# A gated recurrence over columns: 1 − z straight from ScalarE, the state as a product less a product, and one group of matmuls one place later

## The chip, the cores and the metric

The kernel runs on one core of one Trainium2 chip. The metric is the time of one execution in microseconds (us), as the device measures it; the median of several runs counts. A profiled execution is one further run whose every instruction is recorded. Engines are PE (TensorE: matmuls; PEld are its weight loads), DVE (VectorE), ACT (ScalarE), POOL (GpSimd) and SP (SyncE, which issues most of the DMAs).

## What is computed

The input is an image `x` of shape (4, 64, 256, 256): batch, channels, height, width. Layer 0 is a gated convolution block (with Fourier products over 8 × 8 patches) added to `x`. Layer 1 normalizes the result in groups and runs a gated recurrent cell over the columns of the image; its output is added too. The change is in layer 1 only:

```python
def _gru_cell(x, h, w_ih, w_hh, b_ih, b_hh):
    gi = x @ w_ih.T + b_ih
    gh = h @ w_hh.T + b_hh
    i_r, i_z, i_n = jnp.split(gi, 3, axis=-1)
    h_r, h_z, h_n = jnp.split(gh, 3, axis=-1)
    r = jax.nn.sigmoid(i_r + h_r)
    z = jax.nn.sigmoid(i_z + h_z)
    n = jnp.tanh(i_n + r * h_n)
    return (1.0 - z) * n + z * h
...
def step(prev_col, cur_col):
    nb = jnp.concatenate([pad, prev_col, pad], axis=1)
    x = jnp.concatenate([nb[:, :-2], nb[:, 1:-1], nb[:, 2:]], axis=-1)
    new = _gru_cell(x..., cur_col..., w_ih, w_hh, b_ih, b_hh)
    return (new, new)
```

Two things are unusual. What the cell calls `h` is the current column of the normalized image, and what it calls `x` is the previous column's new state with its upper and lower neighbour (three taps). So the 255 steps hang on each other through `w_ih`, while the products with `w_hh` need only the image.

## The kernel before

Layer 0 fills the first 4.37 ms and is not touched. Layer 1 then takes 256 columns `w` in order (the loop at the end of the kernel). All values are fp32. Two images of 64 channels lie on the 128 partitions, and two such pairs lie side by side, so a column is a tile of 128 partitions × 2 × 256 rows.

A column is cut into two ranges of its 256 rows, part 0 and part 1 (`parts`). The border between them moves up by one row with every column, from 144 down to 113, and jumps back every 32 columns. So the three taps of part 0 need only part 0 of the previous column's state; part 1 needs both parts, and at a jump part 0 does too.

`column` issues PE's work. `own` is a product of the column itself with `w_hh`, four matmuls on the four quadrants of the array (eight records in the trace: each fp32 matmul is recorded twice); `taps` is the three products with the previous state, twelve matmuls (24 records). The results lie in four PSUM tags with one buffer each, two banks per buffer, which makes all eight banks: `hr` (r; pshr in the profile), `ni` (the taps' share of n; psni), `hz` (z; pshz), one buffer per range, and `hn` (the column's own share of n; pshn), one buffer for the whole column, which both ranges read. PE's order in a column is: pshn for all 256 rows; then for each range pshr (own, taps), psni (taps), pshz (own, taps).

`state` issues the rest for each range, in this order. ACT: r into tile `g` (sigmoid of pshr), then `normalize` of half a column that is eight columns ahead (`xn<-raw`), then tanh into tile `n`, then z (sigmoid of pshz). DVE: `n` = (pshn + bias) · r (SCALAR_TENSOR_TENSOR n<-pshn), `n` = psni + n, and behind the tanh three steps: g = xn − n, g = g · z, st = g + n. The state `st` is what the next column's taps read. The tiles `g`, `n`, `z` have a pool of two buffers for each range (`gk`).

Program order is kept on every engine (`InOrder`), and each engine takes its queue strictly in order: an instruction that waits holds up all behind it. After a column, POOL adds its state to the image for the output (`add`, raw<-raw,st); SP issues the loads of later columns, the transposed copies `xt<-xn` of the normalized columns, and the stores. ACT computes sigmoid as a function of scale · input + bias, with the sum of two biases in the small tile `b_rz`.

Of the kernel before, what the change touches and what calls it, by code (L numbers as in the profile page):

```python
# [11 lines left out]
AF = mybir.ActivationFunctionType  # L12
ALU = mybir.AluOpType
# [3 lines left out]
B, C, W, H = 4, 64, 256, 256  # L17
# [145 lines left out]
def tile_conv_then_gru(  # L163
# [17 lines left out]
    nc = InOrder(tc, tc.nc)  # L181
# [84 lines left out]
    nc.scalar.dma_start(bias_sb, bias.rearrange("a o n -> (a o) n"))  # L266
    b_rz = const.tile([P, 2], F32, tag="b_rz", name="b_rz")
    nc.vector.tensor_tensor(b_rz, bias_sb[:, 0:2], bias_sb[:, 3:5], ALU.add)

    st1 = const.tile([P, NBLK, 2], F32, tag="st1", name="st1")
    with ExitStack() as s:
# [18 lines left out]
        z = big.tile([P, NP, NS], F32, tag="z", name="z")  # L292
# [424 lines left out]
    with ExitStack() as s:  # L717
        rawp = s.enter_context(tc.tile_pool(name="raw", bufs=3))
        colp = s.enter_context(tc.tile_pool(name="cols", bufs=2))
        gk = s.enter_context(tc.tile_pool(name="gk", bufs=2))  # L720
        ps_g = s.enter_context(tc.tile_pool(name="ps_g", bufs=1, space=PSUM))
        raws, xns, xts, stcols = {}, {}, {}, {}

        def columns(m, w):

            yield m[:, :, w, :].rearrange("(k a) c h -> (a c) k h", k=NPAIR), slice(0, P), 0
            for half in range(2):
                b0 = SLOTS[1][0][half]
                yield m[b0 : b0 + 2, :, w + 1, :].rearrange("b c h -> c b h"), slice(half * C, half * C + C), 1

        def load_columns(w):
            n, i = w // WB, w % WB
            if i == 0:
                raws[n] = rawp.tile([P, 2, WB, H], F32, tag="raw", name=f"raw_{n}")
            for of, at, j in columns(x1, w):
                nc.sync.dma_start(raws[n][at, :, i + j], of)

        def new_columns(n):
            xns[n] = colp.tile([P, 2, WB, H], F32, tag="xn", name=f"xn_{n}")
            xts[n] = colp.tile([P, WB, H], F32, tag="xt", name=f"xt_{n}")  # L740

        def empty_states(n):
            stcols[n] = st = colp.tile([P, 2, WB, H + 2], F32, tag="st", name=f"st_{n}")
            nc.gpsimd.memset(st[:, :, :, 0:1], 0.0)
            nc.gpsimd.memset(st[:, :, :, H + 1 : H + 2], 0.0)

        def normalize(w, slot):
            n, i = w // WB, w % WB
            if i == slot == 0:
                new_columns(n)  # L750
            nc.scalar.activation(
                xns[n][:, slot, i],
                raws[n][:, slot, i],
                AF.Identity,
                bias=sc1[:, w % 2, slot, 0:1],
                scale=sc1[:, w % 2, slot, 1:2],
            )
            if slot and i % 2:

                for half in range(2):  # L760
                    nc.sync.dma_start(
                        xts[n][half * C : (half + 1) * C, i - 1 : i + 1],
                        xns[n][(1 - half) * C : (2 - half) * C, half, i - 1 : i + 1],
                    )

        def add(w):
            n, i = w // WB, w % WB
            nc.gpsimd.tensor_tensor(
                raws[n][:, :, i], raws[n][:, :, i], stcols[n][:, :, i, 1 : H + 1], ALU.add
            )  # L770
            if i % 2:
                for of, at, j in columns(out, w - 1):
                    nc.sync.dma_start(of, raws[n][at, :, i - 1 + j])

        QUARTERS = ((0, 0), (0, 1), (1, 0), (1, 1))
        SKEW = 32

        def parts(w):


            at = H // 2 + SKEW // 2 - (w - 1) % SKEW
            return (0, at), (at, H)

        MAX = H // 2 + SKEW // 2

        def bank_pair(gate, w):
            return ps_g.tile([P, 2, 512], F32, tag=gate, name=f"ps{gate}_{w}")

        def quarters(ps, weights, rhs, start, stop):
            for r, c in QUARTERS:  # L790
                nc.tensor.matmul(
                    ps[c * C : (c + 1) * C, r],
                    lhsT=weights[r * C : (r + 1) * C],
                    rhs=rhs(r, c),
                    start=start,
                    stop=stop,
                    tile_position=(r * C, c * C),
                )

        def column(w):  # L800

            i, xn, xt, st = w % WB, xns[w // WB], xts[w // WB], stcols[(w - 1) // WB]

            def own(ps, gate, h0, h1, stop):

                quarters(
                    ps,
                    wh[:, gate, :],
                    lambda r, c: (xn[:, c] if r == c else xt)[r * C : (r + 1) * C, i, h0:h1],
                    True,  # L810
                    stop,
                )

            def taps(ps, gate, h0, h1, start):
                for t in range(3):
                    quarters(
                        ps,
                        wi[:, 3 * gate + t, :],
                        lambda r, c: st[r * C : (r + 1) * C, c, (w - 1) % WB, h0 + t : h1 + t],
                        start and t == 0,  # L820
                        t == 2,
                    )

            pn = bank_pair("hn", w)[:, :, 0:H]
            own(pn, 2, 0, H, True)
            for part in range(2):
                h0, h1 = parts(w)[part]
                pr, pi, pz = (bank_pair(gate, f"{w}_{part}")[:, :, 0 : h1 - h0] for gate in ("hr", "ni", "hz"))
                own(pr, 0, h0, h1, False)
                taps(pr, 0, h0, h1, False)  # L830
                taps(pi, 2, h0, h1, True)
                own(pz, 1, h0, h1, False)
                taps(pz, 1, h0, h1, False)
                state(w, part, pn[:, :, h0:h1], pr, pi, pz)

        def state(w, part, pn, pr, pi, pz):
            h0, h1 = parts(w)[part]
            i, num = w % WB, h1 - h0
            xn, st = xns[w // WB], stcols[w // WB]
            g = gk.tile([P, 2, MAX], F32, tag=f"g{part}", name=f"g_{w}_{part}")[:, :, 0:num]  # L840
            n = gk.tile([P, 2, MAX], F32, tag=f"n{part}", name=f"n_{w}_{part}")[:, :, 0:num]
            z = gk.tile([P, 2, MAX], F32, tag=f"z{part}", name=f"z_{w}_{part}")[:, :, 0:num]
            nc.scalar.activation(g, pr, AF.Sigmoid, bias=b_rz[:, 0:1], scale=1.0)
            if w + WB < W:
                normalize(w + WB, part)
            nc.vector.scalar_tensor_tensor(n, pn, bias_sb[:, 5:6], g, ALU.add, ALU.mult)
            nc.vector.tensor_tensor(n, pi, n, ALU.add)
            nc.scalar.activation(n, n, AF.Tanh, bias=bias_sb[:, 2:3], scale=1.0)
            nc.scalar.activation(z, pz, AF.Sigmoid, bias=b_rz[:, 1:2], scale=1.0)
            nc.vector.tensor_tensor(g, xn[:, :, i, h0:h1], n, ALU.subtract)  # L850
            nc.vector.tensor_tensor(g, g, z, ALU.mult)
            nc.vector.tensor_tensor(st[:, :, i, 1 + h0 : 1 + h1], g, n, ALU.add)

        for w in range(0, 2 * WB, 2):
            load_columns(w)
        for w in range(WB + 1):
            for slot in range(2):
                normalize(w, slot)
        empty_states(0)
        nc.vector.tensor_copy(stcols[0][:, :, 0, 1 : H + 1], xns[0][:, :, 0])  # L860
        for w in range(W):
            n, i = w // WB, w % WB
            if i == 0 and n + 1 < W // WB:
                empty_states(n + 1)
            if w:
                column(w)
            add(w)
            if i % 2 and w + 2 * WB < W:
                load_columns(w + 2 * WB - 1)
# [54 lines left out]
```

## Time and profile before

| | us |
|---|---|
| median of 3 runs | 5915.67 |
| lowest and highest of them | 5904.98, 5931.4 |
| profiled execution: its own time | 5924.77 |
| profiled execution: span of the trace | 5923.0 |
| first and last DVE step n<-pshn of layer 1, from the start of the span | 4371, 5910 |

Over the whole span PE is busy for 93%, DVE for 69%, ACT for 59% and POOL for 8%; the mean granted TensorE clock is 0.992.

How the lines are read. A row of the timeline has the start from the beginning of the span, the duration (both in us), the engine, the operation, the tile that it writes and those that it reads, the shape, a count, and in brackets the idle time before it and what ended that. All instructions have the line number of one helper (L157), so the tiles' names tell them apart. A row of the waits has who waited for whom, the total in us, the number of times, and the longest. A row of the busy times has the window, its length, then PE, PEld, DVE, ACT and POOL busy time with instruction counts, the granted clock, the share of the DMA engines and GB/s. Matmuls overlap each other, so the pace of PE is read from the starts of successive groups.

### The profile page before, as it was taken

The page shows a single profiled execution, that of the slowest core. Times are in us where ns is not written, and L with a number is a line of the kernel's source. Part 1 is how long each engine was busy: PE and PEld are TensorE (multiplying, and loading weights), DVE is VectorE, ACT ScalarE, POOL GpSimd, SP SyncE. Part 2 cuts the span into 40 slices and gives each one's busy share as a digit, 9 for nine tenths or more (in the row PEclk, how much of TensorE's full clock was granted, in tenths as well). Part 3 has the DMA queues.
Part 4 walks back from the last instruction along what each step waited for, and adds up shares of the span by engine and source line. Part 5 has one row for each costly group of instructions (what it writes and reads, how often), then busy time and mean ns, then how long its engine had stood idle before and what let it go on. Part 6 is the DMA issues. An engine that isn't in the chain of part 4 may idle for free. (4 is left out here: it accounts for less than half of the span.)

```text
span 5923.0 us, 279366 instructions
## 1 busy us (share of the span) xinstructions
PE 5513.2 (93%) x127196; PEld 4736.6 (80%) x127196; DVE 4090.4 (69%) x9592; ACT 3466.3 (59%) x4604; POOL 499.7 (8%) x797
## 2 busy tenths in 40 slices
PE   2999999999999999999999999999979999999998
PEld 1888887888887888778878887887868888888887
DVE  2676776777667777776767776666766666676666
ACT  2556565665655666556566665656645555555555
POOL 0000000000000000000000000000001211121211
PEclk9999999999999999999999999999989999999999
DMA  8455555555555555555555545444454444444442
GB/s 223 132 160 142 154 151 155 152 141 160 151 147 149 157 155 141 147 162 146 153 146 154 145 127 142 133 131 136 123 119 112 113 112 110 113 114 113 111 113 78
DMA packets 561921, 818.09 MB, mean 138 GB/s; under 512 B 41352, under 2 KB 435372, under 8 KB 559676
## 3 DMA queue, kind: packets, MB, share of 16 engines
q1 hardware_dynamic: 520152, 633.59, 39.9%
q0 software_dynamic: 37776, 165.24, 9.5%
q8 instruction: 996, 16.32, 1.2%
q10 hardware_dynamic: 2808, 1.38, 0.1%
q14 instruction: 189, 1.55, 0.1%
HBM read 622.46 MB, written 144.05 MB: 129 GB/s over the span
## 5 line engine op out<-in xcount | busy, mean ns | idle before, releaser
L157 PEld LDWEIGHTS psring<-h,t 100*32 100x32 f32 x40960 | 1334.8, 115 | 300.4 <-issue 176.2
L157 PE MATMUL psring<-h,t 100*32 100x128 f32 x40960 | 1445.7, 274 | 113.0 <-issue 39.4
L157 PE MATMUL psring<-w_sb,xq 64*100 64x128 f32 x24576 | 1396.9, 271 | 58.1 <-POOL xq L157 44.1
L157 PEld LDWEIGHTS psring<-w_sb,xq 64*100 64x100 f32 x24576 | 1352.7, 163 | 117.9 <-issue 48.1
L157 ACT COPY h<-psring 100x1024 f32<-100x1024 f32 x1274 | 1204.0, 1026 | 156.8 <-PE psring L157 150.4
L157 DVE TENSOR_TENSOR pr<-psring,q 128x512 f32<-128x512 f32 (+1 forms) x576 | 463.0, 856 | 299.1 <-PE psring L157 230.8
L157 DVE BATCH_NORM_STATS2 lnst<-z 128x6 f32<-128x64 f32 x4096 | 544.8, 212 | 117.6 <-ACT z L157 117.6
L157 DVE TENSOR_TENSOR z<-z,lnm 128x1024 f32<-128x1024 f32 x512 | 612.6, 1217 | 8.7
L157 ACT COPY q<-psring 128x1024 f32<-128x1024 f32 x256 | 259.2, 1013 | 586.5 <-PE psring L157 351.2
L157 ACT ACTIVATE n<-n,bias_sb 128x288 f32<-128x288 f32 (+7 forms) x510 | 259.8, 509 | 572.7 <-DVE n L157 572.7
L157 ACT COPY z<-psring 128x2048 f32<-128x2048 f32 x128 | 238.9, 1866 | 463.3 <-PE psring L157 458.3
L157 PE MATMUL psring<-pr,g_sb 32*64 32x512 f32 x8192 | 497.5, 602 | 5.9 <-issue 5.7
L157 ACT ACTIVATE y<-psring,ln_sb 128x512 f32<-128x512 f32 x512 | 371.9, 780 | 199.7 <-PE psring L157 196.0
L157 DVE COPY h<-psring 100x1024 f32<-100x1024 f32 x262 | 320.3, 1223 | 193.5 <-PE psring L157 189.4
L157 PE MATMUL psni<-st,wi 64*64 64x144 f32 (+7 forms) x12240 | 440.9, 270 | 7.4 <-issue 6.7
L157 PE MATMUL pshr<-st,wi 64*64 64x144 f32 (+7 forms) x12240 | 434.0, 270 | 13.4 <-DVE st L157 12.9
L157 PE MATMUL pshz<-st,wi 64*64 64x144 f32 (+7 forms) x12240 | 439.4, 270 | 3.9 <-issue 3.5
L157 DVE TENSOR_TENSOR g<-xn,n 128x288 f32<-128x288 f32 (+7 forms) x510 | 217.4, 426 | 325.5 <-ACT n L157 325.5
L157 POOL TENSOR_TENSOR raw<-raw,st 128x512 f32<-128x512 f32 x256 | 303.4, 1185 | 1212.0 <-DVE st L157 522.0
L157 DVE TENSOR_TENSOR y<-psring,y 128x1024 f32<-128x1024 f32 x256 | 312.2, 1220 | 122.1 <-ACT y L157 118.8
L157 PEld LDWEIGHTS pshr<-st,wi 64*64 64x64 f32 x12240 | 362.1, 133 | 16.5 <-issue 16.0
L157 PEld LDWEIGHTS psni<-st,wi 64*64 64x64 f32 x12240 | 363.1, 133 | 14.3 <-issue 11.4
(97 smaller groups left out, 6984.0 us busy)
## 6 DMA issues: line engine op xcount, KB each, us to landing
t<-t_all SPq DMA_DIRECT2D x768, 400.0 KB
xq<-in_xh POOLq DMA_DIRECT2D x128, 800.0 KB, 4.6
xr<-in_x SPq DMA_DIRECT2D x256, 256.0 KB
x<-xr SPq DMA_DIRECT2D x256, 256.0 KB
seen<-in_x POOLq DMA_DIRECT2D x192, 256.0 KB, 4.1
raw<-x SPq DMA_DIRECT2D x128, 256.0 KB
raw<-x SPq DMA_DIRECT2D x256, 128.0 KB
xt<-xn SPq DMA_DIRECT2D x256, 128.0 KB
```

The source lines that it names most:

```text
L157: return self.tc.keep_in_program_order(got(*args, **kwargs))
```

## The change

- ACT computes z' = 1 − z in place of z: the sigmoid of the negated sum (scale −1, and a bias that one more small DVE instruction negates once, at the start).
- ACT's order in a range becomes r, normalize, z', tanh (z' ahead of tanh).
- DVE's last three steps of a range become g = (z' − 1) · xn, which reads no result of the tanh; n = n · z'; st = n − g.
- On PE, pshn is issued behind the two groups of pshr of part 0 and ahead of its psni. The count of PE, DVE and ACT instructions in a column stays as it was. The first DVE step of part 0 now waits for PE as well as for ACT, since pshn is written after pshr.

```diff
     nc.vector.tensor_tensor(b_rz, bias_sb[:, 0:2], bias_sb[:, 3:5], ALU.add)
+    nc.vector.tensor_scalar(b_rz[:, 1:2], b_rz[:, 1:2], -1.0, None, ALU.mult)
...
             pn = bank_pair("hn", w)[:, :, 0:H]
-            own(pn, 2, 0, H, True)
             for part in range(2):
...
                 own(pr, 0, h0, h1, False)
                 taps(pr, 0, h0, h1, False)
+                if part == 0:
+                    own(pn, 2, 0, H, True)
                 taps(pi, 2, h0, h1, True)
...
             nc.vector.tensor_tensor(n, pi, n, ALU.add)
+
+            nc.scalar.activation(z, pz, AF.Sigmoid, bias=b_rz[:, 1:2], scale=-1.0)
             nc.scalar.activation(n, n, AF.Tanh, bias=bias_sb[:, 2:3], scale=1.0)
-            nc.scalar.activation(z, pz, AF.Sigmoid, bias=b_rz[:, 1:2], scale=1.0)
-            nc.vector.tensor_tensor(g, xn[:, :, i, h0:h1], n, ALU.subtract)
-            nc.vector.tensor_tensor(g, g, z, ALU.mult)
-            nc.vector.tensor_tensor(st[:, :, i, 1 + h0 : 1 + h1], g, n, ALU.add)
+            nc.vector.scalar_tensor_tensor(g, z, -1.0, xn[:, :, i, h0:h1], ALU.add, ALU.mult)
+            nc.vector.tensor_tensor(n, n, z, ALU.mult)
+            nc.vector.tensor_tensor(st[:, :, i, 1 + h0 : 1 + h1], n, g, ALU.subtract)
```

## The prediction

> **What bounds it now.** I read the page's chain first, then the waits, then the timeline of one column on each engine, and last the busy times of the stage. Only layer 1's recurrence is touched: 255 columns, which fill the trace from 4371 us to 5910 us.
>
> ```profile
> DVE 17%; PE 6%; ACT 4%; issue 3%; DMA 0%; DVEq 0%; SPq 0%; ACTq 0%; POOLq 0%
> ...
> 5000.00:5300.00 300.00, 279.75 (x9185) 254.74 (x9188) 209.28 (x500) 177.52 (x400) 60.33 (x64) 1.00 0.41 113
> ```
>
> The whole-span chain is mostly DVE although PE is the busiest engine. In the stage (second row: PE, PEld, DVE, ACT, POOL busy, then granted clock) PE is 93% busy, DVE 70%, ACT 59%. The waits name the circle:
>
> ```profile
> ACT n L157 <- DVE n L157: 572.7, 510, 1.9
> DVE g L157 <- ACT n L157: 325.5, 510, 0.9
> PEld pshn L157 <- DVE n L157: 134.3, 227, 1.0
> PE pshn L157 <- DVE n L157: 79.1, 207, 0.7
> ```
>
> Tanh waits for DVE in all 510 ranges, DVE for tanh in all 510, and the first product of a column (pshn) waits for DVE. DVE's timeline, from the second range of one column to the first of the next:
>
> ```profile
> 5071.15 0.48 DVE L157 SCALAR_TENSOR_TENSOR n<-pshn,bias_sb,g 128x262 f32<-128x262 f32 x1
> 5071.73 0.43 DVE L157 TENSOR_TENSOR n<-psni,n 128x262 f32<-128x262 f32 x1
> 5072.80 0.43 DVE L157 TENSOR_TENSOR g<-xn,n 128x262 f32<-128x262 f32 x1 [0.64 <-ACT n L157]
> 5073.34 0.43 DVE L157 TENSOR_TENSOR g<-g,z 128x262 f32<-128x262 f32 x1
> 5073.81 0.43 DVE L157 TENSOR_TENSOR st<-g,n 128x262 f32<-128x262 f32 x1
> 5074.15 0.47 DVE L157 SCALAR_TENSOR_TENSOR n<-pshn,bias_sb,g 128x248 f32<-128x248 f32 x1
> ```
>
> The next range's first DVE step follows the state's last one without a pause, although its r had ended at 5073.73 (last ACT fence: 5073.26 + 0.47). So DVE is a closed ring: five steps and the tanh, start to start 0.58 + 0.53 (to tanh at 5072.26) + 0.54 (tanh to DVE) + 0.54 + 0.47 + 0.34 = 3.00 us for this range, 2.95 with the other one, 5.95 for a column; the starts of this step over all columns have a median distance of 5.95 too. PE follows it:
>
> ```profile
> 5071.68 0.43 PE L157 MATMUL pshn<-xn,wh 64*64 64x256 f32 x1 [0.35 <-DVE n L157]
> ...
> 5072.16 0.27 PE L157 MATMUL pshr<-xn,wh 64*64 64x124 f32 x1
> ...
> 5073.86 0.81 PE L157 MATMUL pshz<-st,wi 64*64 64x124 f32 x24
> 5074.49 0.27 PE L157 MATMUL pshr<-xn,wh 64*64 64x132 f32 x1
> ...
> 5075.40 0.85 PE L157 MATMUL psni<-st,wi 64*64 64x132 f32 x24
> ...
> 5077.62 0.43 PE L157 MATMUL pshn<-xn,wh 64*64 64x256 f32 x1 [0.34 <-DVE n L157]
> ```
>
> From 5071.68 to 5075.40 groups follow each other with nothing between: 3.72 us. What is left of the column (ni 0.68, z's own 0.23 and taps 0.68, by the like groups of the second range) is 1.59. PE needs 5.31 us for a column and takes 5.94. About 0.63 us is slack given back by the wait of pshn.
>
> **The change, part by part.** *State.* The subtraction and its dependent multiply go; in their place stands (z' − 1)·xn, which needs z' = 1 − z and xn but not tanh. Behind the tanh two steps are left. The ring becomes 0.58 + 0.53 + 0.54 + 0.47 + 0.34 = 2.46 us for a range, 4.92 a column, or 5.0 with 0.07 for the second wait that the first range's step now has (PE and ACT; 0.07 is the pause of 0.11 before g<-g,z, which waits for two, less 0.04 before st, which waits for one). The new step runs in DVE's present idle time: DVE can issue 0.34 after the start of n<-psni (5072.07), and tanh's result comes at 5072.80, so 0.73 is free. Its duration has no row. Nearest are 0.48 (the same operation from PSUM), 0.43 (products in SBUF) and 0.52 (the page's smaller groups: the same operation on lnm, 256 elements); I take 0.48. It costs nothing up to 0.8. Uncovered it would cost 0.4 to 0.5 a range, and the ring would be back near 5.9.
>
> *z' before tanh.* A scale of −1 on the same operation costs nothing by these rows. What changes is the queue: tanh and r of the other range stand behind z', which waits for the last product of its range.
>
> ```profile
> 5072.26 0.51 ACT L157 ACTIVATE n<-n,bias_sb 128x262 f32<-128x262 f32 x1 [1.25 <-DVE n L157]
> 5072.68 0.46 ACT L157 ACTIVATE z<-pshz,b_rz 128x262 f32<-128x262 f32 x1
> 5073.26 0.47 ACT L157 ACTIVATE g<-pshr,b_rz 128x248 f32<-128x248 f32 x1
> 5075.24 0.50 ACT L157 ACTIVATE n<-n,bias_sb 128x248 f32<-128x248 f32 x1 [1.02 <-DVE n L157]
> ```
>
> The first range's pshz ends at 5073.86 + 0.81 = 5074.67 and its tanh starts at 5075.24: 0.57 of idle ACT for a step that issues in 0.36. So z' fits ahead of tanh now.
>
> *n of the column itself behind r.* Alone it buys nothing, since DVE sets the pace. Together with the shorter ring, the wait for the PSUM pair that pshn shares between columns gets 0.85 us of PE work (r's products) in front of it.
>
> *What is late next: PE.* I lay a column of 5.31 us out from r's start (0): r ends issuing at 0.85, n 1.33, ni 1.97, z 2.81, second r 3.72, ni 4.40, z 5.31; a result is usable about 0.25 later (a group of taps is 0.81 long while the next starts after 0.63, and 0.07 passes before ScalarE starts where r waits for it alone). z' starts 3.06, tanh 3.42, product 3.96, state 4.43 to 4.85; the second range's first step 4.77, n 5.35 to 5.78, tanh 5.92 (behind z' at 5.56), product 6.46, state 6.93 to 7.36, which is 2.05 of the next column; its first step follows at 1.96, n at 2.54 to 2.97, ahead of tanh at 3.42. It closes with 0.35 to spare. PE never waits: state of the first range needed at 5.52, there at 4.85; of the second at 3.04, there at 2.05; n's pair needed at 6.16, read by 5.24.
>
> *Elsewhere.* The extra step on b_rz (0.16 us, once) follows DVE's 44.3 us wait for the bias. No DMA moves; SP's own waits in the stage are 423 us for POOL and 373 for ACT, so its queue stands a column 0.6 shorter. POOL's addition (1.1 to 1.3 us of a column) starts 0.13 after the second state's end, so it can overlap the first range's new step. Had that to stand until the addition's end, 1.41 after the state's, the product would start 0.24 late and the ring be 5.24, still under PE's 5.31. [...]
>
> *Sum.* 5.95 − 5.31 = 0.64 over 254 column distances: 163 us. Not all comes in. Some fifty PE groups start 0.2 to 1.4 us late in the middle of a product, about 24 us in all, of which the slack now swallows some 17: the distances sum to 1536 against 254 × 5.955 = 1513, and seven columns where the ranges' border jumps back (every 32; 2.2 us waiting for the second state, before and after) take 16 of that 23. Minus 17, and 2 for the transposed copy's rare waits: 144 to 146 us. Own time 5924.8 − 146 = 5779; it lies 9 above the median of the three runs (5915.7), so I predict 5770.
>
> **Rivals.** *PE does not reach its own pace (0.12):* the ring stays at 5.4 to 5.5, if the new step takes 0.8 or more or stands behind POOL, or handoffs cost more than shown. The 0.35 to spare speaks against it, the missing row for it. 5.45 a column: 36 us less, 5806.
>
> *The new step is not hidden (0.05):* if z' always comes too late, DVE does it behind tanh: 2 × (2.46 + 0.48) = 5.88, a gain of 18 us, 5898: no change. The 0.57 us of idle ACT speaks against it.
>
> *Clock (0.08, slower):* TensorE at half its clock, as here:
>
> ```profile
> 4563.69:4567.10 3.41, 3.41 (x66) 3.41 (x60) 0.97 (x2) 1.26 (x3) 0.74 (x1) 0.50 0.13 40
> ```
>
> Such windows follow PE's longest pauses (the 2.2 us of a border jump), three in this stage. With PE as the bound a column takes 5.31 / c: the gain is gone at a mean clock of 0.89 and it turns to a loss below. A third of the time at half clock, c = 0.83, gives 6.4 a column: +114 us, 6030. Against it: 1.00 in the stage, and in layer 0 with PE as dense as it would be here. [...]
>
> **Numbers.** Forecast 0.75, its own range 5742 (all 163 come in, less the 11 by which the lowest run lies under the median) to 5800; partial 0.12; no change 0.05; slower 0.08. Up to 5865 the range holds the partial case too, as far as 5.7 a column. A measurement of this kernel can tell about 0.5% from no change.
>
> **What would show it.** Right: the distance of columns 5.3 to 5.4; pshn's wait for DVE gone; DVE's new step inside its old idle time, two steps after tanh; ACT n waiting for its turn behind z rather than for DVE; PE near 98% in the stage. Wrong: columns near 5.9 with the new step behind tanh, pshr waiting for st in ordinary columns, or a clock below 0.95.

## The result: 0.8% faster, under a third of what was forecast

| | us |
|---|---|
| before, median of 4 runs (lowest, highest) | 5914.34 (5904.98, 5931.4) |
| after, median of 4 runs (lowest, highest) | 5872.74 (5863.04, 5877.1) |
| ratio after to before, 95% interval | 0.9921 (0.9902 to 0.9941) |
| profiled execution of after: its own time, its span | 5869.95, 5868.2 |
| mean distance of columns in layer 1, before and after | 6.048, 5.870 |

The medians lie 42 us apart; 146 were forecast. (The ratio is the one on record; the quotient of the two medians is 0.9930, inside its interval.) The two profiled executions differ by 55 us. The 254 distances between the first DVE steps of successive columns sum to 1536 us before and 1491 after, so 45 of the 55 lie in the recurrence; 9 more lie ahead of layer 1, which started at 4371 us before and at 4362 after, where only one small step at the start was changed. The granted clock is 0.994.

The chain of the page of after, by engine, and below it the busy times of the stage (columns as for before):

```profile
PE 33%; issue 2%; DMA 1%; DVE 1%; ACT 1%; SPq 0%; POOLq 0%; ACTq 0%; DVEq 0%
```

```profile
5000.00:5300.00 300.00, 277.99 (x9328) 264.73 (x9324) 211.55 (x508) 182.29 (x408) 61.73 (x66) 1.00 0.42 116
```

PE has taken DVE's place on the chain, as the prediction said. But in the 300 us it worked off only 1.5% more records than before (9328 and 9324 against 9185 and 9188), and its busy time even fell, from 279.75 to 277.99 us: the forecast wanted columns of 5.48 us in the mean in place of 6.05, 9% less. The waits of after, from 4400 to 5850 us:

```profile
ACT z L157 <- PE pshz L157: 505.0, 493, 2.7
...
PE pshz L157 <- issue: 28.7, 53, 1.2
PE pshr L157 <- issue: 28.6, 59, 1.2
...
PE psni L157 <- issue: 21.6, 30, 1.7
PE pshr L157 <- DVE st L157: 13.4, 7, 1.9
...
ACT n L157 <- DVE n L157: 6.0, 26, 0.6
```

The old circle is open. Tanh waits for DVE 26 times instead of at every range, pshn waits for DVE once (0.2 us), and ScalarE stands in z' and waits for PE's last product. PE waits for a state only at the seven jumps of the border. What it does wait for is "issue", that is, for nothing that the profile can name: 79 us in these three rows. In the same window of before they came to 14:

```profile
PE psni L157 <- issue: 6.7, 14, 0.9
PE pshz L157 <- issue: 5.8, 13, 1.2
...
PE pshr L157 <- issue: 1.2, 3, 0.5
```

The timeline of DVE and ACT in one range:

```profile
5067.51 0.50 DVE L157 SCALAR_TENSOR_TENSOR n<-pshn,bias_sb,g 128x272 f32<-128x272 f32 x1
5068.10 0.44 DVE L157 TENSOR_TENSOR n<-psni,n 128x272 f32<-128x272 f32 x1
5068.79 0.49 ACT L157 ACTIVATE z<-pshz,b_rz 128x272 f32<-128x272 f32 x1 [1.08 <-PE pshz L157]
5069.17 0.51 ACT L157 ACTIVATE n<-n,bias_sb 128x272 f32<-128x272 f32 x1
5069.31 0.44 DVE L157 SCALAR_TENSOR_TENSOR g<-z,xn 128x272 f32<-128x272 f32 x1 [0.76 <-ACT z L157]
5069.72 0.44 DVE L157 TENSOR_TENSOR n<-n,z 128x272 f32<-128x272 f32 x1
5070.20 0.44 DVE L157 TENSOR_TENSOR st<-n,g 128x272 f32<-128x272 f32 x1
```

The second row of DVE ends at 5068.54, tanh starts at 5069.17, and between them lies z' with its wait for PE (1.08 us). The new step (0.44) runs beside the tanh, and two steps follow. All of this is the picture forecast. Only PE isn't at its pace.

### The profile page after: what moved, and what is told of

It is laid out like the page before. It is cut to its first block, busy times and chain, and to the rows that moved or that the text cites. A ratio compares the mean times of both kernels' runs of the same rounds, so it can differ in the third digit from the quotient of the medians.

```text
span 5868.2 us, 278629 instructions
## 1 busy us (share of the span) xinstructions
PE 5479.9 (93%) x127196; PEld 4762.6 (81%) x127196; DVE 4080.5 (70%) x9593; ACT 3475.4 (59%) x4604; POOL 500.8 (9%) x797
## 3 DMA queue, kind: packets, MB, share of 16 engines
q10 hardware_dynamic: 2808, 1.38, 0.1%
## 5 line engine op out<-in xcount | busy, mean ns | idle before, releaser
L157 ACT ACTIVATE z<-pshz,b_rz 128x288 f32<-128x288 f32 (+7 forms) x510 | 242.6, 476 | 519.8 <-PE pshz L157 519.7
L157 PE MATMUL pshr<-st,wi 64*64 64x144 f32 (+7 forms) x12240 | 510.5, 270 | 34.9 <-issue 20.9
L157 PE MATMUL psni<-st,wi 64*64 64x144 f32 (+7 forms) x12240 | 510.4, 270 | 24.4 <-issue 22.4
L157 PE MATMUL pshz<-st,wi 64*64 64x144 f32 (+7 forms) x12240 | 510.8, 270 | 23.1 <-issue 21.9
L157 PEld LDWEIGHTS psni<-st,wi 64*64 64x64 f32 x12240 | 446.5, 133 | 45.5 <-issue 34.4
L157 PEld LDWEIGHTS pshr<-st,wi 64*64 64x64 f32 x12240 | 422.3, 133 | 52.3 <-issue 49.5
L157 PEld LDWEIGHTS pshz<-st,wi 64*64 64x64 f32 x12240 | 424.9, 133 | 37.3 <-issue 36.4
L157 DVE SCALAR_TENSOR_TENSOR g<-z,xn 128x288 f32<-128x288 f32 (+7 forms) x510 | 218.4, 428 | 311.9 <-ACT z L157 310.0
```

The source lines that it names most:

```text
L157: return self.tc.keep_in_program_order(got(*args, **kwargs))
```

## The cause: PE's instructions arrive in blocks

PE's timeline has short pauses in the middle of a product, where the profile names nothing that the next matmul waits for:

```profile
4408.66 0.65 PE L157 MATMUL psni<-st,wi 64*64 64x120 f32 x16
4409.91 0.33 PE L157 MATMUL psni<-st,wi 64*64 64x120 f32 x4 [0.59 <-issue]
```

A group of taps has 24 records; this one stops after its 17th (one lies ahead of the 16 shown) and goes on 0.86 us after the last start. The same happens at other places in other columns. The page of after has what to set beside this: the engines' counts of instructions and the queues' counts of packets.

```profile
PE 5479.9 (93%) x127196; PEld 4762.6 (81%) x127196; DVE 4080.5 (70%) x9593; ACT 3475.4 (59%) x4604; POOL 500.8 (9%) x797
```

```profile
q8 instruction: 996, 16.32, 1.2%
```

PE and PEld together have 254,392 records; 996 transfers of 16.4 KB at 256 records each are 254,976. Queue q8 carries PE's program: its count follows PE's records from kernel to kernel (1012 in split_n, 988 in pair_n, 941 in whole_ni, below). The stage has, from 4400 to 5850 us:

```profile
q8 instruction: 354, 5.80, 1.7%
```

In the records of the single transfers these 354 are 4.09 us apart in the mean, with 256 PE records (matmuls and weight loads) between two starts. Counting a pause as a distance of over 0.25 us between the starts of two PE records, there are 218 (156 us; the text on record of few_stores has 155); 215 of them end 1.0 to 2.0 us after the end of a q8 transfer, at a median of 1.39 us, where chance would put about a quarter there. In the pause shown it is 1.38 us.

The arithmetic: a column has 92 fp32 matmuls, each two matmul and two weight-load records, so 368 records or 1.4375 blocks. At the array's pace of 5.31 us a column (the estimate from the starts of before's groups), a block would have to come every 256 · 5.31 / 368 = 3.69 us. It came every 4.09: 1.4375 · 4.09 = 5.88 us a column, measured 5.87. That product alone proves nothing, since a column's records must arrive in a column's time whatever sets the pace (before: 1.4375 · 4.21 = 6.05). What says more is what is left without the pauses: less an ordinary spacing of 0.06 us for each (nine in ten of all distances are shorter) they are 143 us, and the other 1307 us of the window for 354 blocks are 3.69 us a block, the array's pace. So the pauses account for the whole difference. That the blocks cause them is tested by changing the records and the array's work separately, in the experiments.

The round trip can be read from the pauses. Behind these 215 pauses the next transfer starts no earlier than 1.05 us after PE resumes (median 1.50); a transfer takes 1.09 us in the mean, and the median pause ends 1.39 us after one. That adds up to 3.5 us with the shortest lag and to 4.0 with the median one. Single blocks do come faster: 28% of the distances lie under 3.69 us, but the mean doesn't. No data packet of q1 was in flight at the start of 83 of these transfers; there the median lag was 1.15 us. Where packets were, it was 1.69.

In the texts on record, **F** is this theory: PE gets a block of 256 records every 4 us or so, and the number of records sets the column. **P**, its rival, has PE at the end of its array work and its hand-offs, so that array time taken away or added shows in full and the number of records doesn't matter. **R** is a ring through the states that is still closed. One more rival has no letter: a fixed time that PE needs for each record, wherever the instructions are. The counts of records alone can't tell it from F; the pauses can (narrow, below).

## The experiments

Ratios are to the kernel before, on the same chip, with 95% intervals. "Against after" is the difference to 0.9921, times 5914 us; with both intervals it is uncertain by some 17 us. Means of block and column are from the one profiled execution of each.

| kernel | ratio | 95% | records a column | us a block | us a column |
|---|---|---|---|---|---|
| before | 1 | | 368 | 4.21 | 6.05 |
| after | 0.9921 | 0.9902 to 0.9941 | 368 | 4.09 | 5.87 |
| state_alone | 0.9932 | 0.9913 to 0.9952 | 368 | 4.12 | 5.91 |
| pn_alone | 1.0005 | 0.9991 to 1.0019 | 368 | | 6.09 |
| split_n | 1.0042 | 1.0025 to 1.0059 | 384 | 4.11 | 6.14 |
| pair_n | 0.9876 | 0.9856 to 0.9896 | 360 | 4.12 | 5.79 |
| narrow | 0.9965 | 0.9945 to 0.9985 | 368 | 4.14 | 5.93 |
| lag2 | 0.9899 | 0.9883 to 0.9914 | 368 | 4.06 | 5.83 |
| few_stores | 0.9812 | 0.9781 to 0.9843 | 368 | 3.93 | 5.65 |
| before_few_stores | 1.0005 | 0.9994 to 1.0016 | 368 | | |
| more_stores | 0.9936 | 0.9917 to 0.9955 | 368 | 4.08 | 5.86 |
| whole_ni | 0.9974 | 0.9960 to 0.9988 | 312 | 4.92 | 5.99 |

**Which part brings the gain.** state_alone is after with pshn at the front of the column again:

```diff
+            own(pn, 2, 0, H, True)
             for part in range(2):
...
-                if part == 0:
-                    own(pn, 2, 0, H, True)
```

> The state's three steps and the order of ScalarE as in the changed kernel, but pshn first in the column as before. Theory F (PE now runs out of instructions: it takes them in blocks of 256 records, 16 KB each, on queue q8, and a block comes every 4.09 us on average, so the 368 records of a column take 5.87 us): PE is the bound here too, 5860 to 5890 us, as with both edits. Theory P (PE's own pace or the handoffs set the 5.87 us): the pair of pshn is free at 5.24 us of a column by my layout, so it again costs little: 5860 to 5900. If the place of pshn carried the gain: 5900 or more.

pn_alone is before with pshn moved behind pshr of part 0, and nothing else (the same lines the other way round).

> Only pshn moved behind the products of r of the first range; the state's steps as before. Both theories: DVE's ring of 5.95 us a column still sets the pace, so no gain; with the second wait of the first range's step up to 0.07 us a column longer: 5910 to 5935 us. A gain of 30 or more would say that the ring was not the bound before.

The new order of the state brings the gain, 0.9932; the move of pshn alone brings nothing, 1.0005. Whether the move adds something to the state's change (0.9921 against 0.9932) is within the intervals and stays open.

**More records, the same work.** split_n issues pshn in two halves of 128 rows instead of one of 256, with the same number of columns through the array and 16 records more:

```diff
-                    own(pn, 2, 0, H, True)
+                    own(pn[:, :, 0 : H // 2], 2, 0, H // 2, True)
+                    own(pn[:, :, H // 2 : H], 2, H // 2, H, True)
```

> The changed kernel with each matmul of pshn (256 columns wide) cut into two of 128: the same array work, 16 more PE records in a column, 384 in place of 368 (4.3% more). Theory F: the time of a column grows with the count, 5.87 to 6.12 us, 64 us in all: 5925 to 5940 us. Theory P: the array's work is the same, at most 0.03 us a column for one more group: 5870 to 5882 us.

It lost all that the change had won and more: 1.0042, 72 us against after. F priced 16 records at 64 us, P at 9 or less. The block came at 4.11 us, as in after; only the column has more of them.

**Fewer records, the same work.** pair_n computes pshn for two columns with one set of matmuls 512 wide (the first column alone), into the same two PSUM banks:

```diff
+        lead, k = w % 2 == 0 or w == 1, 1 if w == 1 else 2
+        if lead:
+            pairs[0] = bank_pair("hn", w)[:, :, 0 : k * H].rearrange("p c (k h) -> p c k h", h=H)
+        pn = pairs[0][:, :, 0 if lead else 1]
...
-                if part == 0:
-                    own(pn, 2, 0, H, True)
+                if lead and part == 0:
+                    quarters(
+                        pairs[0],
+                        wh[:, 2, :],
+                        lambda r, c: (xn[:, c] if r == c else xt)[r * C : (r + 1) * C, i : i + k, :],
+                        True,
+                        True,
+                    )
```

> The changed kernel with pshn computed for two columns at once (512 columns wide, every second column): the same array work, 8 PE records fewer a column on average (360 of 368, 2.2%). Theory F: 5.87 to 5.74 us a column, 32 us less than the changed kernel, 0.9865 of the kernel before. Theory P: no change, 0.992.

0.9876, 27 us against after, where F said 32 and P nothing. pair_n is the fastest version of the whole computation here: 5840.78 us beside 5912.92 for the kernel before on its chip.

**The same records, less work.** narrow lets the taps of r and z multiply only the first 64 rows of each range. It leaves part of these products out; the number of matmuls stays, and the array has less work, by the estimate on record 1.31 us in a column:

```diff
-                taps(pr, 0, h0, h1, False)
+                taps(pr[:, :, 0:64], 0, h0, h0 + 64, False)
...
-                taps(pz, 1, h0, h1, False)
+                taps(pz[:, :, 0:64], 1, h0, h0 + 64, False)
```

> The changed kernel, but the taps of r and z cover only the first 64 rows of each range (left out: the other rows' share; ScalarE and DVE read as much as before). Record counts stay at 368 a column, PE's array work falls by 2 x (0.635 - 0.33) + 2 x (0.68 - 0.33) = 1.31 us to 4.0 us a column, under the ring's 5.0. Theory F: a block of 256 records still takes some 3.95 to 4.09 us, so a column 5.65 to 5.87 us: 0 to 60 us less than the changed kernel. Theory P (the array's work is the limit): the ring sets the pace, 5.0 to 5.1 us, about 200 us less.

0.9965: not faster but slower, by some 26 us against after. Its waits in the window from 4400 to 5850 us, and the busy times of the stage:

```profile
PE pshr L157 <- issue: 116.1, 106, 2.4
PE pshz L157 <- issue: 111.3, 111, 2.4
...
PE psni L157 <- issue: 93.2, 88, 2.4
```

```profile
5000.00:5300.00 300.00, 227.54 (x9340) 208.92 (x9341) 212.18 (x505) 180.09 (x405) 60.35 (x63) 0.99 0.42 114
```

The matmuls that are gone from the array have become waits for issue, 321 us in the three rows where after has 79. PE's busy time fell by 50 us in the 300, and its count of records did not move: 18,681 against 18,652 in after. The pauses are now 383 (447 us), and 340 of them end 1.0 to 2.0 us after a block's end. P, which had to gain some 200 us, is out. So is a fixed time per record: without the pauses (424 us less their ordinary spacing) PE takes 2.92 us for a block here (88 records in a us) and 3.69 in after (69), where the means over the whole window are 62 and 63; it is quicker as soon as the instructions are there. F's own band (no loss) was missed as well: the block came at 4.14 us. Why it came a little later than in after isn't explained.

**The state of two columns ago.** lag2 lets the taps read the state of the column before the previous one. It computes another recurrence, with the same instructions and a column more of slack:

```diff
-            i, xn, xt, st = w % WB, xns[w // WB], xts[w // WB], stcols[(w - 1) // WB]
+            i, xn, xt, st = w % WB, xns[w // WB], xts[w // WB], stcols[max(w - 2, 0) // WB]
...
-                        lambda r, c: st[r * C : (r + 1) * C, c, (w - 1) % WB, h0 + t : h1 + t],
+                        lambda r, c: st[r * C : (r + 1) * C, c, max(w - 2, 0) % WB, h0 + t : h1 + t],
```

> The changed kernel, but the taps read the state of two columns ago (another recurrence; left out: the wait for the last state). Every instruction, transfer and shape stays. Theory F: PE is not held by the state, only the seven border jumps go: 10 to 20 us less than the changed kernel. Rival R (the ring through the state and its handoffs holds PE at 5.87 in place of 5.31 us a column): some 140 us less.

0.9899, 13 us against after, in F's band of 10 to 20, though with the 17 us above it can't be told from nothing. R asked for 140 and is out. PE's wait for st at the jumps (13.4 us in after) is gone, and the distances of columns sum to 9 us less; its three rows for issue are 82.5 us, as in after (79). The column takes 5.83 us, so it is no ring through the state that holds it at 5.87.

**What sets the block's time.** few_stores leaves out layer 1's stores of the output, but for the first and last two columns, to see whether the transfers of the program compete with the data:

```diff
-        if i % 2:
+        if i % 2 and (w < 2 or w > W - 2):
```

> The changed kernel with the stores of layer 1's output left out, all but the first and last two columns (256 KB a column of about 640 KB that the DMA queues move). No engine's work changes but SP's. Theory F: the blocks of instructions share the DMA engines with these transfers, so they come sooner; the column falls to 5.4 to 5.6 us, 5760 to 5805 us in all, and PE's pauses of over 250 ns (155 us in the changed kernel) fall to under half. Theory P: nothing that PE waits for has changed, 5865 to 5880 us.

0.9812: 65 us against after. The median of 5820 lies 15 us above F's band, on a chip where before too took 15 us longer than in the runs of the result, and the pauses fell to 97 us, not under half of after's 156; the direction is F's, the size a little short. The block came at 3.93 us instead of 4.09. before_few_stores leaves the same stores out of the kernel before, where the ring sets the pace:

> The kernel before (DVE's ring as the bound), with the same stores left out as in few_stores. Theory F: PE's pauses for instructions lie under the slack of 0.63 us a column, so at most the visible few go: 0 to 15 us less than the kernel before. If it gains as much as the changed kernel did from the same cut (some 60 us), the stores slow something else than PE's instructions, and F loses that support.

1.0005: nothing. So leaving the stores out gained 65 us where PE waited for its supply, and nothing where the ring set the pace. more_stores goes the other way and writes each store a second time, into a spare tensor:

```diff
+    spare = dram.tile([B, C, W, H], F32, tag="spare", name="spare")
...
+            for of, at, j in columns(spare, w - 1):
+                nc.sync.dma_start(of, raws[n][at, :, i - 1 + j])
```

> The changed kernel with each store of layer 1's output issued once more, into a spare tensor (256 KB more a column). Theory F: blocks of instructions come later by about what few_stores gained (3.93 in place of 4.09 us a block), so some 4.2 to 4.3 us and a column of 6.05 to 6.2 us: 45 to 85 us longer than the changed kernel. Theory P: no change.

This was a miss: 0.9936, within the intervals of after, with 4.08 us a block, although the DMA share of the stage rose from 0.42 to 0.57. The share of time without a q1 packet in flight went from 36% to 20% (few_stores: 55%). Between PE's resuming and the next transfer, median lags of 1.15 us without and 1.63 with packets in flight are there in this run as well. So a block does start later when data is in flight, but the time isn't a line through the amount of data: the median lag over all pauses is 1.15 us in few_stores, 1.50 in after and 1.48 here. Why fewer stores gain 1.1% and more cost nothing stays open.

**Far fewer records.** whole_ni is pair_n with the taps of n for the whole column at once (256 wide): 312 records, 56 fewer than after. For that, z's products move ahead of pshn and of these taps.

```diff
+            pi_all = bank_pair("ni", w)[:, :, 0:H]
...
-                taps(pi, 2, h0, h1, True)
                 own(pz, 1, h0, h1, False)
                 taps(pz, 1, h0, h1, False)
...
+                if part == 0:
+                    taps(pi_all, 2, 0, H, True)
+                pi = pi_all[:, :, h0:h1]
```

> pair_n with the taps of n for the whole column at once (256 wide, behind z of the first range): 312 records a column in place of 360, the same array work. Theory F alone: 312 / 256 x 4.1 = 5.0 us for the records, so the array's 5.31 us becomes the limit, if nothing else waits. But these taps need both ranges' last state at some 1.7 to 2.2 us of a column, and by the same layout as in the prediction the second one is there at about 2.4: 0.2 to 0.7 us of waiting. Together 5.5 to 5.8 us a column, 0.970 to 0.986 of the kernel before, PE's pauses for instructions nearly gone and a wait of psni for st in most columns. Theory P: the added wait makes it slower than pair_n, 0.99 or more.

A miss: 0.9974, 31 us slower than after. Its waits in the window from 4400 to 5850 us:

```profile
ACT n L157 <- DVE n L157: 569.2, 484, 2.1
...
PEld psni L157 <- DVE st L157: 153.2, 234, 1.0
...
PE psni L157 <- DVE st L157: 58.8, 113, 0.8
```

The block now came every 4.92 us: PE asked for it more slowly than it had come in after (4.09). The wait of PEld psni for issue is 6.9 us in this run, where after has 33.3. In its place PE's joint taps wait for the second range's state, and tanh waits for DVE in 484 ranges as in before. The records no longer bind, and the way through both states does. The kernel changed two things at once, the joining of the taps and their place behind z, and no run here parts them; what the waits show is that a product that needs both states stood waiting in nearly every column.

## Why the prediction was wrong, step by step

- **DVE's ring: right.** Two steps behind the tanh, the new step hidden (mean 0.428 us where 0.48 was taken), z' at 0.476 us in the mean where z took 0.456 (the scale of −1 had been put at nothing), tanh waiting behind z', pshn's wait gone. before_few_stores and pn_alone show the other side: with the ring closed, the stores and PE's order changed nothing (1.0005 both).
- **PE next: right, as an engine.** PE leads the chain; ACT z' waits for it 493 times.
- **"PE never waits": wrong; this is the step that failed.** 5.31 us is what the array needs by the starts of before's groups; in after PE does come to that pace between the pauses (3.69 us a block). The prediction had seen "some fifty PE groups" that "start 0.2 to 1.4 us late in the middle of a product, about 24 us in all", and carried them over as a fixed toll, 17 us of it new. They were mostly PE's supply already: of 57 pauses in the trace of before that don't end at pshn, 44 end 1.0 to 2.0 us after a q8 transfer. In after, with the ring open, 212 don't end at pshn, and 210 of these lie as far behind a transfer; that PE's faster demand makes more of them is a reading of these two counts. All 218 pauses of after are 156 us; less an ordinary spacing of 0.06 us for each that is 143, and less the jumps' 13 about 130. The term was 24 and measured 130.
- **The sum.** The prediction put the 254 distances at 1536 − 144 = 1392 us, 5.48 in the mean; they are 1491, 5.87. The 99 us between are that term's 106 (130 less 24), within what the two counts differ by. The step from 163 to 146 us was sound except for this.
- **The rivals.** "PE does not reach its own pace" came true by its name and not by its mechanism: it laid the fault on the ring (5.4 to 5.5 us a column), and its 5806 was 67 us too low. The uncovered step, priced at 5898, did not occur. The clock stayed at 0.994, and the stage has one window of half clock (5488.8 to 5492.2 us) where before had three. Each of the four begins within 0.7 us of the end of the pause at a jump of the border (2.19 to 2.55 us), but four of before's seven jumps and six of after's have none behind them, so what brings them isn't shown. In after's window 24 taps 144 wide take 1.74 us and right behind it 0.94; 49 matmul records start in its 3.41 us, and at the 33 a us of the next 47 us that would be 1.5 us of work, so it cost some 1.9 us by this estimate.
- **"What would show it."** Of its five signs of being right three came (pshn, the new step, ACT n). The distance of columns of 5.3 to 5.4 and PE near 98% did not. Its sign of the wrong case, "columns near 5.9", came without its cause, the new step behind the tanh. The signs had no row for PE waiting on nothing.

The trace of before held a warning: 345 q8 transfers, 4.21 us apart in the mean with PE waiting for the ring, against the 3.69 that the forecast needed from them. Nothing there showed 3.69 kept up for long: the best ten distances in a row have a mean of 3.96. But PE asked for no more there, so that trace couldn't say what the supply would give when pressed.

## What to carry to other kernels

Before you forecast that TensorE will run at its array's pace, count its records (368 for the 92 fp32 matmuls of a column here, four for each) and divide by the time that you hope for: here the stage stayed at 61 to 65 records in a us in every kernel that waited for its instructions, with matmuls from 64 to 512 wide. (before, held by its ring, ran at 61 too, so the rate alone doesn't tell a bound; the pauses do.) Pauses in the middle of a product with "issue" as releaser are not a toll to be carried over, since they grew here from 57 to 212 (those that don't end at pshn) when the other waits went; match their ends against the ends of the instruction queue's transfers. What helped here was fewer and wider matmuls (pair_n, 27 us), but not where they joined what a dependence needs apart (whole_ni, 31 us slower than after).

## What the hardware showed that was not expected

- **Instruction supply.** PE's blocks of 256 records came 4.09 to 4.14 us apart in the mean under this traffic, whether the array has, by the estimate from before's groups, 5.31 us of work in 368 records (after), 5.31 in 384 (split_n) or 4.00 in 368 (narrow). With the stores left out it is 3.93. From the end of such a pause to the next transfer's start it was never under 1.05 us in after: only after PE had gone on did the next block start to come.
- **DVE and GpSimd.** In lag2 DVE's new step falls on POOL's addition far more often (84 times, against 37 in after). The timeline of one such place:

```profile
5054.69 1.09 POOL L157 TENSOR_TENSOR raw<-raw,st 128x512 f32<-128x512 f32 x1
5054.87 1.22 DVE L157 SCALAR_TENSOR_TENSOR g<-z,xn 128x272 f32<-128x272 f32 x1 [1.06 <-ACT z L157]
5056.01 0.43 DVE L157 TENSOR_TENSOR n<-n,z 128x272 f32<-128x272 f32 x1
```

The step takes 1.22 us and ends 0.3 us after POOL's. The 84 steps that overlap such an addition take 0.758 us in the mean, the 426 others 0.429; POOL's own additions stay at 1.09 to 1.30. The 46 steps of over 0.55 us start at most 0.94 us after the start of POOL's addition, and all end 0.25 to 0.30 us after its end, as if held until POOL is nearly through. POOL was first in all of these; this run shows no case where DVE was. In after all but one of the 37 overlapping steps start 0.97 us or more after the start of POOL's addition, near its end; their mean is 0.434 us, the longest 0.809, so it cost next to nothing there.
